# Separate counts for the last group, five parts of one-hots, and 16-bit one-hots of units in a graph-attention and expert kernel

## The chip, the core and the metric

The kernel runs on one core of a Trainium2 chip. The core has five engines that run their own instruction streams side by side: TensorE (matrix products, PE in the profile, with its weight loads as PEld), VectorE (DVE), ScalarE (ACT), GpSimd (POOL) and SyncE (SP, which issues DMAs). Each engine executes its stream in order and waits on semaphores for the others. Products are written to PSUM, everything else works in SBUF, 128 partitions wide. The metric is the device time of one execution in microseconds (us); lower is better.

## What is computed

There are N = 6250 rows of 256 features. The first half is one step of a graph attention, the second a mixture of 8 experts with the best two of each row:

```python
x = x + gnn(layernorm(x))      # per row: 4 heads, softmax over heads, sum over heads
t = layernorm(x)               # the tokens
logits = t @ router_w.T        # [6250, 8]
rw, re = top_k(softmax(logits), 2); rw = rw / rw.sum(-1)
out = t
for e in range(8):
    h = gelu(t @ w1[e] + b1[e])
    out = out + combine[:, e:e+1] * (h @ w2[e] + b2[e])
x = x + out
```

`combine[n, e]` is the share of expert e in row n, and 0 where e isn't one of the two. A row therefore needs only two of the eight experts.

## The kernel before

**First stage.** The rows are cut into 49 tiles of 128, kept in five groups (`GROUPS`: 10, 10, 9, 10 and 10 tiles). For every tile TensorE computes the features of the graph step (`features`, L483) and a table look-up (`look_up`, L508). For every group VectorE then computes the attention (`attend_1` to `attend_3`) and the routing (`route`, L597), which finds the two best experts of each row. Two experts make one of 28 pairs; `mine_all` (L158, 16-bit) holds a one-hot of the pair of each row, 28 values for each tile.

**Sorting.** Rows are then sorted by pair, so that each slice of 128 sorted rows needs few experts. The place of a row is the number of rows of earlier pairs, plus the rows of its pair in earlier tiles, plus those in earlier partitions of its own tile. `rank(g)` (L644) does the last two for a group on TensorE: products of one-hots with a strictly triangular matrix (`before_b`) and with ones (`ones_b`), added up in PSUM, 28 columns for each tile and 28 more for the sum over the whole group. `ranked(g)` (L662) reads these on VectorE: it adds the group's sum to the running `counts`, picks each row's own pair (a product with the one-hot and a sum over pairs), and puts the result into `rank_all`. For groups 0 to 3 this is hidden in the first stage. The last group, z, comes when the first stage is over: L851 to L861 scale its heads on ScalarE (`scaled_heads`), route it, rank it, sum its heads on TensorE (`summed_heads`, whose result ScalarE copies out of PSUM), store its rows to the table in DRAM and call `ranked(z)`.

From L864 on everything is a chain over engines. VectorE turns the counts into `ends`, `starts` and `base` (the first place of each pair in each group), multiplies the base with the one-hots (`ms`, one product for each group), sums over pairs (`place`) and adds `rank_all`. The place is split into a slice (place / 128) and a lane (place % 128).

**Inverting.** The kernel needs for each slice and lane which row stands there. `places(t0, t1)` (L899) makes, for some tiles, 16-bit one-hots of the slice (49 values for each tile) and of the lane (128 values) on VectorE, and two copies of the slice's one-hot, times the row's partition (ScalarE, L906) and times its tile (VectorE, L907). The tile index is innermost in these arrays, with a pitch of 50 values. `placed(t0, t1)` (L910) multiplies them on TensorE, one product of 98 columns for each tile, added up in `pi`. This goes in three parts: tiles 0 to 7, 8 to 23 and 24 to 48, the last with a column of padding. From `pi` VectorE makes `held_by` (L960), the row that each place holds, and GpSimd gathers the rows by it (`fetch`, L982).

**Units.** In parallel VectorE finds which experts each slice takes (`has`, `takes`, `upto`; one small product `pu` between tiles 35 and 36 of `pi`), and numbers the pairs of slice and expert: 125 units. `is_unit` (L954) is a one-hot of each unit's number, 8 experts by 125 units. Sixteen products `pf` (L1001), for the slice and for the expert of each unit and over the 8 experts each, turn it into two lists of 125 numbers. TensorE executes them behind the last product of `pi`. From them come the integer lists from which the engines load registers (`name_units`, L1115).

**Expert loop.** From L1214 on, each of the 125 units takes one slice through one expert: `fill` loads w1 of the expert from DRAM, `first` multiplies and applies the gelu, `second` multiplies with w2 and adds to `acc`. `norm` normalises gathered rows and `turn_slice` transposes them ahead of the loop. `keep_on(26)` (L1005) are 26 products whose result isn't used, on TensorE between pf and the first transpose of a slice.

The order of instructions on every engine is the program's order (a manual schedule); nothing reorders it.

Of the kernel before, what the change touches and what calls it, by code (L numbers as in the profile page):

```python
# [9 lines left out]
FP = mybir.dt.float32  # L10
BF = mybir.dt.bfloat16
I32 = mybir.dt.int32
AF = mybir.ActivationFunctionType
ALU = mybir.AluOpType
# [8 lines left out]
def kernel(  # L23
# [37 lines left out]
    nc = tc.nc  # L61
    N, D = x.shape
    H, OC = attn_l.shape
    NE, _, F = w1.shape
    P = 128
    NT = -(-N // P)
# [3 lines left out]
    GROUPS = [(0, 10), (10, 10), (20, 9), (29, 10), (39, 10)]  # L70
    NG = len(GROUPS)
# [12 lines left out]
    NPAIR = len(PATH)  # L84
    TS = 128
    NS = -(-N // TS)
    NU = 2 * NS + NPAIR - 1
# [22 lines left out]
    ps = ctx.enter_context(tc.tile_pool(name="ps", bufs=2, space=PSUM))  # L110
# [3 lines left out]
    def wide(v, n):  # L114
        return v.rearrange("p (t k) -> p t k", k=1).to_broadcast([v.shape[0], v.shape[1], n])

    def long(v, n):
        return v.rearrange("p (t k) -> p t k", t=1).to_broadcast([v.shape[0], n, v.shape[1]])

    def group(g):  # L120
        return slice(GROUPS[g][0], sum(GROUPS[g]))
# [8 lines left out]
    count_up = const.tile([128, 128], FP, name="count_up")  # L130
# [16 lines left out]
    ones_b = held.tile([128, 128], BF, name="ones_b")  # L147
# [9 lines left out]
    counts = held.tile([P, NG + 1, NPAIR], FP, name="counts")  # L157
    mine_all = held.tile([P, NT, NPAIR], BF, name="mine_all")  # L158
    rank_all = held.tile([P, NT], FP, name="rank_all")
    outside = held.tile([P, 1], FP, name="outside")  # L160
# [3 lines left out]
    NTE = NT + NT % 2  # L164
# [15 lines left out]
    work = early.enter_context(tc.tile_pool(name="work", bufs=2))  # L180
    small = early.enter_context(tc.tile_pool(name="small", bufs=2))
# [39 lines left out]
    for of, pattern, k in ((count_up, [[1, 128]], 0), (number, [[0, 1]], 1)):  # L221
        nc.gpsimd.iota(
            of, pattern=pattern, base=0, channel_multiplier=k,
# [73 lines left out]
    pf = ps.tile([128, NE + 2 * H], FP, name="pf", tag="m")  # L297
# [39 lines left out]
    for c in range(DC):  # L337
        pa = ps.tile([128, 2, H], FP, name="pa", tag="m")
        for k in range(H // 2):
            nc.tensor.matmul(  # L340
                pa, turned_w[2 * c + k], terms[:, k, :, :],
                start=(k == 0), stop=(k == H // 2 - 1),
# [43 lines left out]
    def pair_tables():  # L386

        nc.vector.tensor_scalar(before_b, count_up, number, None, ALU.is_gt)
        nc.vector.tensor_scalar(valid, number, float(LAST), None, ALU.is_lt)

        nc.vector.tensor_scalar(
            outside, number, float(LAST), float(2 * NS * TS), ALU.is_ge, ALU.mult
        )


        for e in range(NE):
            nc.vector.memset(order[:, e : e + 1], 2.0 ** (NE - e))


        one_of = small.tile([P, 2, NPAIR], FP, name="one_of", bufs=1)  # L400
        for i, (a, b) in enumerate(PATH):
            for k, e in enumerate((a, b)):
                nc.vector.memset(one_of[:, k, i : i + 1], float(e))
        for i, (a, b) in enumerate(PATH):
            nc.vector.memset(pairs[:, i : i + 1], 2.0 ** (NE - a) + 2.0 ** (NE - b))

        other = small.tile([NS, NE, NPAIR], FP, name="other", tag="mr", bufs=1)
        for k, to in enumerate((member, other)):
            nc.vector.tensor_tensor(
                to,  # L410
                one_of[:NS, k : k + 1, :].to_broadcast([NS, NE, NPAIR]),
                wide(count_up[:NS, :NE], NPAIR),
                ALU.is_equal,
            )
        nc.vector.tensor_tensor(member, member, other, ALU.add)
        for k in range(2):
            nc.vector.tensor_scalar(
                edge[:, k : k + 1], number[:NS], float(TS), float(k * TS), ALU.mult, ALU.add
            )
# [160 lines left out]
    def summed_heads(g, i, n):  # L580
        pv = ps.tile([P, n, OC], FP, name="pv2", tag="m")
        for h in range(H):
            nc.tensor.matmul(
                pv, ident, pxss[g][:, i : i + n, h * HB : h * HB + OC],
                start=(h == 0), stop=(h == H - 1),
            )
        nc.scalar.copy(xs[g][:, i : i + n, U : U + OC], pv)
# [4 lines left out]
    ranks = {}  # L592

    def store_rows(g):
        nc.sync.dma_start(table_v[:, group(g), :], xs[g])
# [45 lines left out]
            )  # L641
        yield

    def rank(g):  # L644


        n, mine = GROUPS[g][1], mine_all[:, group(g), :]
        pk = ps.tile([P, n + 1, NPAIR], FP, name="rank", tag="r")
        nc.tensor.matmul(pk[:, 0, :], before_b, mine[:, 0, :], start=True, stop=True)
        nc.tensor.matmul(  # L650
            pk[:, 1:, :], ones_b, mine[:, 0:1, :].to_broadcast([P, n, NPAIR]),
            start=True, stop=False,
        )
        nc.tensor.matmul(pk[:, 1:n, :], before_b, mine[:, 1:, :], start=False, stop=False)
        for i in range(1, n):
            nc.tensor.matmul(
                pk[:, i + 1 :, :], ones_b, mine[:, i : i + 1, :].to_broadcast([P, n - i, NPAIR]),
                start=False, stop=(i == n - 1),
            )
        ranks[g] = pk  # L660

    def ranked(g):  # L662
        n, pk = GROUPS[g][1], ranks.pop(g)
        nc.vector.tensor_tensor(
            counts[:, g + 1, :], counts[:, g, :], pk[:, n, :], ALU.add
        )
        mr = small.tile([P, n, NPAIR], FP, name="mr", tag="mr", bufs=1)
        nc.vector.tensor_tensor(mr, pk[:, :n, :], mine_all[:, group(g), :], ALU.mult)
        nc.vector.tensor_reduce(rank_all[:, group(g)], mr, AX.X, ALU.add)
        if g == NG - 1:  # L670
            nc.vector.tensor_tensor(
                rank_all[:, NT - 1 :], rank_all[:, NT - 1 :], outside, ALU.add
            )

# [72 lines left out]
    steps_b = mid.tile([P, TS, CUT], BF, name="steps_b", bufs=1)  # L749
# [49 lines left out]
    for k, (g, b, n) in enumerate(FEATURES):  # L799
# [3 lines left out]
        for j in range(n):  # L803
            i = b + j
# [28 lines left out]
    z = NG - 1  # L833
    n = GROUPS[z][1]
# [9 lines left out]
    warm = small.tile([P, 1], FP, name="warm", bufs=1)  # L844
    nc.scalar.activation(warm, exs[z][:, 0, :1], AF.Gelu)
    rank(z - 1)
    keep_on(8)
    ranked(z - 1)
    attend_2(z)

# [3 lines left out]
    scaled_heads(z, m, n - m)  # L854
    for _ in route(z):
        pass
    rank(z)
    summed_heads(z, 0, m)
    summed_heads(z, m, n - m)
    store_rows(z)  # L860
    ranked(z)  # L861


    count = counts[:, NG, :]  # L864
# [4 lines left out]
    base = small.tile([P, NG, NPAIR], FP, name="base", bufs=1)  # L869
    nc.vector.tensor_tensor(base, counts[:, :NG, :], long(starts, NG), ALU.add)  # L870
    ms = held.tile([P, NT, NPAIR], FP, name="ms", tag="x1")
    for g in range(NG):
        nc.vector.tensor_tensor(
            ms[:, group(g), :], mine_all[:, group(g), :],
            base[:, g : g + 1, :].to_broadcast([P, GROUPS[g][1], NPAIR]), ALU.mult,
        )
    place = small.tile([P, NT], FP, name="place", bufs=1)
# [21 lines left out]
    def places(t0, t1):  # L899

        at, n = slice(t0, t1), t1 - t0
        for to, k, of in ((of_slice, NS, slice_b), (of_lane, TS, lane_b)):
            nc.vector.tensor_tensor(
                to[:, :, at], steps_b[:, :k, :n], long(of[:, at], k), ALU.is_equal
            )
        nc.scalar.activation(by[:, 0, :, at], of_slice[:, :, at], AF.Identity, scale=number)  # L906
        nc.vector.tensor_tensor(  # L907
            by[:, 1, :, at], of_slice[:, :, at], long(count_b[:, at], NS), ALU.mult
        )
    def placed(t0, t1):  # L910
        for t in range(t0, t1):
            nc.tensor.matmul(
                pi, of_lane[:, :, t], by[:, :, :, t], start=(t == 0), stop=(t == NT - 1)
            )

    places(0, 8)
    placed(0, 8)
    places(8, 24)
    placed(8, 24)
    places(24, NTE)  # L920
    placed(24, 36)

    has = small.tile([NS, NPAIR], FP, name="has", bufs=1)
    nc.vector.tensor_scalar(has, ends[:NS], edge[:, 0:1], None, ALU.is_gt)
# [7 lines left out]
    takes = small.tile([NS, NE], FP, name="takes", bufs=1)  # L932
# [4 lines left out]
    nc.vector.tensor_copy(every, upto[:, NE - 1 :])  # L937
    pu = ps.tile([NS, 1], FP, name="pu", tag="r")
    nc.tensor.matmul(pu, before_b[:NS, :NS], every, start=True, stop=True)
    placed(36, NT)  # L940


    fields = small.tile([NS, 2, NE], BF, name="fields", bufs=1)
# [4 lines left out]

    unit = small.tile([NS, NE], FP, name="unit", bufs=1)
    nc.vector.tensor_scalar(unit, upto, pu, float(2 * NU - 1), ALU.add, ALU.add)  # L950
    nc.vector.scalar_tensor_tensor(
        unit, takes, -2.0 * NU, unit, op0=ALU.mult, op1=ALU.add
    )
    is_unit = work.tile([NS, NE, NU], BF, name="is_unit", tag="tT", bufs=4)  # L954
    nc.vector.tensor_tensor(
        is_unit, long(count_up[:NS, :NU], NE), wide(unit, NU), ALU.is_equal
    )
    part_of = small.tile([TS, NS], FP, name="part_of", bufs=1)
    nc.vector.tensor_copy(part_of, pi[:, 0, :])
# [38 lines left out]
    pf = ps.tile([1, 2, NU], FP, name="pf2", tag="r")  # L998
    for k in range(2):
        for e in range(NE):  # L1000
            nc.tensor.matmul(  # L1001
                pf[:, k, :], fields[:, k, e : e + 1], is_unit[:, e, :],
                start=(e == 0), stop=(e == NE - 1),
            )
    keep_on(26)  # L1005
# [8 lines left out]
    for k, of in ((0, 0), (1, 2)):  # L1014
# [4 lines left out]
        op0=ALU.mult, op1=ALU.add,  # L1019
# [194 lines left out]
    for u in range(NU + LAG + 1):  # L1214
# [11 lines left out]
        k, step = divmod(u, 4)  # L1226
# [46 lines left out]
```

## Time and profile before

| | us |
|---|---|
| median of three runs | 416.77 (415.42 to 417.92) |
| the profiled execution, its own time | 419.29 |
| span of its profile | 417.4 |
| TensorE busy | 379.0 (91% of the span) |
| VectorE busy | 306.6 (73%) |
| ScalarE busy | 240.3 (58%) |
| GpSimd busy | 203.1 (49%) |

A busy share is an average over stages. The first stage ends at about 131 us on the profile's time axis, the sorting, inverting and numbering of units lie between 131 and 171 us, and the expert loop takes the rest. In a line of the timeline stand the start in us, the duration in us, the engine, the line of the kernel, the operation, what it writes and reads, the shapes and the number of instructions merged into the line; the bracket at the end is the idle time before it and what ended it. In the chain of waits each piece of time is given to the engine that the end of the run had to wait for. Granted clock is the share of TensorE's full clock that the chip's throttle let through.

### The profile page before, as it was taken

Reading aid. Unit: us, or ns where it says so; the run is one execution under the profiler, and the core shown is the slowest. Engines: PE = TensorE matmul, PEld = TensorE weight load, DVE = VectorE, ACT = ScalarE, POOL = GpSimd, SP = SyncE. Lnnn points to the kernel's source line nnn. Section 1 sums busy time; section 2 is a strip of 40 time slices with the busy share of each in tenths; the row PEclk is TensorE's granted clock in tenths of the full one; section 3 lists DMA queues with packets and bytes.
Section 4 is the critical chain, followed back from the end, with each engine's and each line's share of the span. In section 5 each row is a group of like instructions: output and inputs, shape, how many; then the busy total and the mean of one; then the engine's idle time right before and its main releaser. Section 6 shows DMA issues by size and latency. Waiting matters only on the chain.

```text
span 417.4 us, 9987 instructions
## 1 busy us (share of the span) xinstructions
PE 379.0 (91%) x2599; PEld 327.3 (78%) x2599; DVE 306.6 (73%) x1089; ACT 240.3 (58%) x703; POOL 203.1 (49%) x244
## 2 busy tenths in 40 slices
PE   5999999979894679789999999999999999999990
PEld 4777887767672455679999999999997999999990
DVE  4989839898678795467977877887796887465551
ACT  3477877666573830557667676666765766333330
POOL 0068888899602004444424666766746634233222
PEclk9599999999898676899999999999999999999996
DMA  6974222639823033765667777677777756666520
GB/s 188 355 256 144 77 79 92 239 117 292 270 105 166 0 165 91 230 190 166 198 188 195 206 218 225 220 227 226 224 207 216 202 169 185 192 187 187 165 73 23
DMA packets 53898, 74.66 MB, mean 179 GB/s; under 512 B 7686, under 2 KB 48250, under 8 KB 52948
## 3 DMA queue, kind: packets, MB, share of 16 engines
q1 hardware_dynamic: 46028, 52.45, 40.0%
q0 software_dynamic: 7248, 21.29, 17.2%
q8 instruction: 24, 0.39, 0.4%
q10 hardware_dynamic: 568, 0.27, 0.2%
q14 instruction: 30, 0.25, 0.2%
HBM read 59.13 MB, written 14.87 MB: 177 GB/s over the span
## 4 chain that ended last, share of the span: by engine, by line
PE 50%; POOL 2%; issue 2%; DMA 2%; DVE 1%; ACT 1%; POOLq 0%; DVEq 0%; SPq 0%; ACTq 0%
PE ph L1164 25%; PE py L1180 23%; PE pt L1110 2%; DMA w<-in_L_ffn_w_dram 1%; POOL xr L986 1%; DVE acc L1187 1%; DMA xr<-table,held_by 1%; POOL nm L1067 1%; POOLq L1268 0%; ACT tokT L1111 0%; DVE stats L1061 0%; DVEq L1124 0%; SPq L1152 0%; ACT acc L1087 0%; POOL out_dram L1191 0%
## 5 line engine op out<-in xcount | busy, mean ns | idle before, releaser
L1164 PEld LDWEIGHTS ph<-tokT,w 128*128 128x128 f32 x1000 | 131.5, 193 | 12.5 <-ACT tokT L1111 6.5
L1164 PE MATMUL ph<-tokT,w 128*128 (+1 forms) x1000 | 133.5, 277 | 3.9 <-ACT tokT L1111 3.8
L1180 PE MATMUL py<-big,hid 128*128 x500 | 128.6, 380 | 0.0
L1171 ACT ACTIVATE hid<-ph,b_cols 128x128 f32<-128x128 f32 x250 | 78.4, 364 | 76.8 <-PE ph L1164 76.6
L1180 PEld LDWEIGHTS py<-big,hid 128*128 128x128 f32 x500 | 85.5, 191 | 6.9 <-DVE acc L1187 0.2
L1187 DVE SCALAR_TENSOR_TENSOR acc<-py,shares,acc 128x256 f32 (+1 forms) x125 | 60.5, 484 | 28.0 <-PE py L1180 17.6
L986 POOL DMA_INDIRECT xr<-table,held_by x49 | 49.2, 1004 | 65.0 <-DVE held_by L960 31.6
L1191 POOL DMA_INDIRECT out_dram<-acc,held_out x49 | 50.9, 1039 | 55.2 <-DVE acc L1187 39.7
L1187 DVE SCALAR_TENSOR_TENSOR acc<-big,shares,acc (+1 forms) x125 | 60.1, 481 | 10.5 <-issue 5.2
L487 PE MATMUL px<-w_sb,tT 128*128 128x293 f32 x196 | 56.1, 420 | 0.0
L1077 ACT ACTIVATE tok<-xr,nm 128x256 f32<-128x256 f32 x49 | 29.3, 599 | 33.0 <-DMA w<-in_L_ffn_w_dram 16.0
L487 PEld LDWEIGHTS px<-w_sb,tT 128*128 128x128 f32 x196 | 35.1, 193 | 7.5 <-issue 0.3
L238 POOL DMA_INDIRECT big<-in_x_dram,dst_sb x31 | 34.0, 1097 | 7.3 <-issue 5.9
L495 ACT COPY pxs<-px 128x293 f32<-128x293 f32 x49 | 19.8, 404 | 23.1 <-PE px L487 22.1
L253 ACT COPY tT<-pt 128x512 f32<-128x512 f32 (+2 forms) x56 | 27.1, 528 | 9.6 <-PE pt L249 9.3
L1051 DVE TENSOR_TENSOR xr<-xr 128x512 f32<-128x512 f32 (+1 forms) x25 | 17.2, 690 | 17.0 <-issue 17.0
L1087 ACT ACTIVATE acc<-xr,nm 128x256 f32<-128x256 f32 x49 | 29.1, 596 | 0.0
L1066 POOL TENSOR_SCALAR mv<-mv 128x2 f32<-128x2 f32 (+1 forms) x25 | 5.7, 228 | 35.5 <-DVE mv L1063 34.0
L238 POOL DMA_INDIRECT xd_own<-in_x_dram,dst_sb x18 | 19.1, 1061 | 4.4 <-issue 3.2
L516 PE MATMUL pl<-al_sb,high 128*128 128x196 bf16 x147 | 18.8, 249 | 2.0 <-DVE ag L524 2.0
L1110 PE MATMUL pt<-ident,tok 128*128 128x128 f32 x98 | 19.0, 276 | 1.2 <-ACT tok L1077 1.2
L1067 POOL TENSOR_TENSOR nm<-mv,half_c 128x2 f32<-128x2 f32 (+1 forms) x25 | 18.4, 735 | 2.1
(221 smaller groups left out, 496.1 us busy)
## 6 DMA issues: line engine op xcount, KB each, us to landing
w<-in_L_ffn_w_dram SPq DMA_DIRECT2D x125, 256.0 KB, 3.1
table<-x SPq DMA_DIRECT2D x4, 1685.0 KB
x<-in_x_dram SPq DMA_DIRECT2D x10, 512.0 KB, 9.7
big<-in_L_ffn_w_dram SPq DMA_DIRECT2D x2, 1024.0 KB
high<-highs SPq DMA_DIRECT2D x1, 1568.0 KB
table<-x SPq DMA_DIRECT2D x1, 1516.5 KB
big<-in_L_ffn_b_dram SPq DMA_DIRECT2D x1, 1024.0 KB
xr<-table,held_by POOLq DMA_INDIRECT x49
```

What stands on the lines that cost most here:

```text
L238: nc.gpsimd.indirect_dma_start(out=xd(t), out_offset=None, in_=x[:, :], in_offset=bass.IndirectOffsetOnAxis(ap=dst_sb[:, t : t + 1], axis=0),)
L253: nc.scalar.copy(tT, pt)
L487: nc.tensor.matmul(px, blocks[c][:, k * P : (k + 1) * P], w_sb[:, c, :], start=(c == 0), stop=(c == DC - 1),)
L986: nc.gpsimd.indirect_dma_start(out=xr[:, i, :], out_offset=None, in_=table[:, :], in_offset=bass.IndirectOffsetOnAxis(ap=held_by[:, s0 + i ...
L1077: nc.scalar.activation(tok[:, i, :], xr[:, i, :D], AF.Identity, bias=bias[:, i : i + 1], scale=scale[:, i : i + 1],)
L1087: nc.scalar.activation(acc[:, s * D : (s + 1) * D], xr[:, i, :D], AF.Identity, bias=bias[:, i : i + 1], scale=more[:, i : i + 1],)
L1110: nc.tensor.transpose(pt[:, c, :], tok[:, c * 128 : (c + 1) * 128], ident)
L1164: nc.tensor.matmul(ph[:, j, :], w[:, c * F + j * 128 : c * F + (j + 1) * 128], tokT[:, bass.ds(rows_at + c * TS, TS)], start=(c == 0), sto ...
L1171: nc.scalar.activation(hid[:, j, :], ph[:, j, :], AF.Gelu, bias=b1_cols[:, :, j][:, bass.ds(at_act[u][0], 1)])
L1180: nc.tensor.matmul(py, hid[:, j, :], we2[:, j, bass.ds(at_pe[u][1], D)], start=(j == 0), stop=(j == FC - 1),)
L1187: nc.vector.scalar_tensor_tensor(to, y, share, to, op0=ALU.mult, op1=ALU.add)
L1191: nc.gpsimd.indirect_dma_start(out=ends_at[s][:, :], out_offset=bass.IndirectOffsetOnAxis(ap=held_out[:n, s : s + 1], axis=0), in_=acc[:n, ...
```

## The change

Three things are changed, all between the end of the first stage and the expert loop.

1. **Counts and ranks of the last group.** A new function `all_of` adds up the one-hots of the last group's ten tiles with ten products of 28 columns of their own. `rank` gets an argument `end`; with 0 it leaves out the sum over the whole group, which makes every product with ones 28 columns shorter and drops the last. In place of `ranked(z)` VectorE adds the new sum to the counts. The ranks stay in PSUM: in the loop that makes `ms`, the last group's `base` is added to them, and the sum is multiplied with the one-hot, so that the sum over pairs yields both at once. The last group's columns of `rank_all` are set at the start, to 0 and, for the last tile, to `outside`.
2. **Five parts.** The one-hots of places are made and used in parts of 5, 6, 8, 11 and 19 tiles (20 with the padding) instead of 8, 16 and 25. The small product `pu` comes after tile 37 instead of 35.
3. **One-hots of units.** `unit` is written as 16-bit values, `is_unit` has the expert innermost instead of the unit, and is made by comparing two 16-bit operands (`steps_b`, a table that counts up and that the places use already). The products `pf` read every eighth value of it.

```diff
--- before.py
+++ after.py
@@ -392,6 +392,9 @@
             outside, number, float(LAST), float(2 * NS * TS), ALU.is_ge, ALU.mult
         )
 
+        nc.vector.memset(rank_all[:, group(NG - 1)], 0.0)
+        nc.vector.tensor_copy(rank_all[:, NT - 1 :], outside)
+
 
         for e in range(NE):
             nc.vector.memset(order[:, e : e + 1], 2.0 ** (NE - e))
@@ -641,23 +644,33 @@
             )
         yield
 
-    def rank(g):
+    def rank(g, end=1):
 
 
         n, mine = GROUPS[g][1], mine_all[:, group(g), :]
-        pk = ps.tile([P, n + 1, NPAIR], FP, name="rank", tag="r")
+        pk = ps.tile([P, n + end, NPAIR], FP, name="rank", tag="r")
         nc.tensor.matmul(pk[:, 0, :], before_b, mine[:, 0, :], start=True, stop=True)
         nc.tensor.matmul(
-            pk[:, 1:, :], ones_b, mine[:, 0:1, :].to_broadcast([P, n, NPAIR]),
+            pk[:, 1:, :], ones_b, mine[:, 0:1, :].to_broadcast([P, n + end - 1, NPAIR]),
             start=True, stop=False,
         )
         nc.tensor.matmul(pk[:, 1:n, :], before_b, mine[:, 1:, :], start=False, stop=False)
-        for i in range(1, n):
+        for i in range(1, n + end - 1):
             nc.tensor.matmul(
-                pk[:, i + 1 :, :], ones_b, mine[:, i : i + 1, :].to_broadcast([P, n - i, NPAIR]),
-                start=False, stop=(i == n - 1),
+                pk[:, i + 1 :, :], ones_b,
+                mine[:, i : i + 1, :].to_broadcast([P, n + end - 1 - i, NPAIR]),
+                start=False, stop=(i == n + end - 2),
             )
         ranks[g] = pk
+
+    def all_of(g):
+        n = GROUPS[g][1]
+        pk = ps.tile([P, NPAIR], FP, name="all", tag="r")
+        for i in range(n):
+            nc.tensor.matmul(
+                pk, ones_b, mine_all[:, GROUPS[g][0] + i, :], start=(i == 0), stop=(i == n - 1)
+            )
+        return pk
 
     def ranked(g):
         n, pk = GROUPS[g][1], ranks.pop(g)
@@ -667,10 +680,6 @@
         mr = small.tile([P, n, NPAIR], FP, name="mr", tag="mr", bufs=1)
         nc.vector.tensor_tensor(mr, pk[:, :n, :], mine_all[:, group(g), :], ALU.mult)
         nc.vector.tensor_reduce(rank_all[:, group(g)], mr, AX.X, ALU.add)
-        if g == NG - 1:
-            nc.vector.tensor_tensor(
-                rank_all[:, NT - 1 :], rank_all[:, NT - 1 :], outside, ALU.add
-            )
 
 
 
@@ -854,11 +863,12 @@
     scaled_heads(z, m, n - m)
     for _ in route(z):
         pass
-    rank(z)
+    of_z = all_of(z)
+    rank(z, 0)
     summed_heads(z, 0, m)
     summed_heads(z, m, n - m)
     store_rows(z)
-    ranked(z)
+    nc.vector.tensor_tensor(counts[:, NG, :], counts[:, z, :], of_z, ALU.add)
 
 
     count = counts[:, NG, :]
@@ -870,8 +880,17 @@
     nc.vector.tensor_tensor(base, counts[:, :NG, :], long(starts, NG), ALU.add)
     ms = held.tile([P, NT, NPAIR], FP, name="ms", tag="x1")
     for g in range(NG):
+        of = mine_all[:, group(g), :]
+        if g == z:
+
+            mr = small.tile([P, n, NPAIR], FP, name="mr", tag="mr", bufs=1)
+            nc.vector.tensor_tensor(
+                mr, ranks.pop(z), base[:, z : z + 1, :].to_broadcast([P, n, NPAIR]), ALU.add
+            )
+            nc.vector.tensor_tensor(ms[:, group(z), :], mr, of, ALU.mult)
+            continue
         nc.vector.tensor_tensor(
-            ms[:, group(g), :], mine_all[:, group(g), :],
+            ms[:, group(g), :], of,
             base[:, g : g + 1, :].to_broadcast([P, GROUPS[g][1], NPAIR]), ALU.mult,
         )
     place = small.tile([P, NT], FP, name="place", bufs=1)
@@ -913,12 +932,12 @@
                 pi, of_lane[:, :, t], by[:, :, :, t], start=(t == 0), stop=(t == NT - 1)
             )
 
-    places(0, 8)
-    placed(0, 8)
-    places(8, 24)
-    placed(8, 24)
-    places(24, NTE)
-    placed(24, 36)
+
+    for t0, t1 in ((0, 5), (5, 11), (11, 19), (19, 30)):
+        places(t0, t1)
+        placed(t0, t1)
+    places(30, NTE)
+    placed(30, 38)
 
     has = small.tile([NS, NPAIR], FP, name="has", bufs=1)
     nc.vector.tensor_scalar(has, ends[:NS], edge[:, 0:1], None, ALU.is_gt)
@@ -937,7 +956,7 @@
     nc.vector.tensor_copy(every, upto[:, NE - 1 :])
     pu = ps.tile([NS, 1], FP, name="pu", tag="r")
     nc.tensor.matmul(pu, before_b[:NS, :NS], every, start=True, stop=True)
-    placed(36, NT)
+    placed(38, NT)
 
 
     fields = small.tile([NS, 2, NE], BF, name="fields", bufs=1)
@@ -948,12 +967,13 @@
 
     unit = small.tile([NS, NE], FP, name="unit", bufs=1)
     nc.vector.tensor_scalar(unit, upto, pu, float(2 * NU - 1), ALU.add, ALU.add)
+    unit_b = small.tile([NS, NE], BF, name="unit_b", bufs=1)
     nc.vector.scalar_tensor_tensor(
-        unit, takes, -2.0 * NU, unit, op0=ALU.mult, op1=ALU.add
+        unit_b, takes, -2.0 * NU, unit, op0=ALU.mult, op1=ALU.add
     )
-    is_unit = work.tile([NS, NE, NU], BF, name="is_unit", tag="tT", bufs=4)
+    is_unit = work.tile([NS, NU, NE], BF, name="is_unit", tag="tT", bufs=4)
     nc.vector.tensor_tensor(
-        is_unit, long(count_up[:NS, :NU], NE), wide(unit, NU), ALU.is_equal
+        is_unit, steps_b[:NS, :NU, :NE], long(unit_b, NU), ALU.is_equal
     )
     part_of = small.tile([TS, NS], FP, name="part_of", bufs=1)
     nc.vector.tensor_copy(part_of, pi[:, 0, :])
@@ -999,7 +1019,7 @@
     for k in range(2):
         for e in range(NE):
             nc.tensor.matmul(
-                pf[:, k, :], fields[:, k, e : e + 1], is_unit[:, e, :],
+                pf[:, k, :], fields[:, k, e : e + 1], is_unit[:, :, e],
                 start=(e == 0), stop=(e == NE - 1),
             )
     keep_on(26)
```

## The prediction

> **What bounds the kernel now.** I first read the shares of the chain that ended last: 50% of the span is TensorE, nearly all of it the expert loop from 170.75 us on, which the change leaves alone. So the change can only move the moment at which that loop starts. The timeline of the stretch before it (139 to 171 us), engine by engine, says what sets that moment.
>
> ```profile
> PE 50%; POOL 2%; issue 2%; DMA 2%; DVE 1%; ACT 1%; POOLq 0%; DVEq 0%; SPq 0%; ACTq 0%
> ```
>
> VectorE after the last group's products:
>
> ```profile
> 141.34 0.18 DVE L664 TENSOR_TENSOR counts<-counts,rank 128x28 f32<-128x28 f32 x1 [1.51 <-PE rank L656]
> 141.44 0.44 DVE L668 TENSOR_TENSOR mr<-rank,mine_all 128x280 f32<-128x280 f32 x1
> ...
> 142.48 0.27 DVE L866 TENSOR_TENSOR_SCAN ends<-counts,zero 128x28 f32<-128x28 f32 x1
> ...
> 148.02 0.69 DVE L903 TENSOR_TENSOR of_lane<-steps_b,part 128x1024 bf16<-128x1024 bf16 x1
> ...
> 157.44 1.19 DVE L955 TENSOR_TENSOR is_unit<-count_up,unit 49x1000 bf16<-49x1000 f32 x1
> 159.54 0.21 DVE L959 COPY part_of<-pi 128x49 f32<-128x49 f32 x1 [0.91 <-PE pi L912]
> ...
> 161.31 0.47 DVE L1008 TENSOR_SCALAR which<-pf 1x125 f32<-1x125 f32 x2 [1.31 <-PE pf L1001]
> ...
> 166.37 0.42 DVE L1051 TENSOR_TENSOR xr<-xr 128x256 f32<-128x256 f32 x1 [1.43 <-issue]
> ```
>
> VectorE waits for TensorE at both late steps (0.91 us for pi, 1.31 us for pf). From 161.31 on nothing but its own work and a register load leads to 166.37, then norm, tok, tokT and the loop. So **the end of pf sets the loop's start**, not the gathers (the first is issued at 160.28). TensorE:
>
> ```profile
> 139.62 0.18 PE L649 MATMUL rank<-mine_all,before_b 128*128 128x28 bf16 x1 [4.57 <-DVE mine_all L637]
> ...
> 141.15 6.02 PE L583 MATMUL pv<-pxs,ident 128*128 128x320 f32 x16
> 149.03 1.68 PE L912 MATMUL pi<-by,of_lane 128*128 128x98 bf16 x8 [1.86 <-DVE by L907]
> 151.12 5.70 PE L912 MATMUL pi<-by,of_lane 128*128 128x98 bf16 x28 [0.40 <-DVE by L907]
> 156.75 0.20 PE L939 MATMUL pu<-every,before_b 49*49 49x1 bf16 x1
> 156.88 2.62 PE L912 MATMUL pi<-by,of_lane 128*128 128x98 bf16 x13
> 159.43 1.84 PE L1001 MATMUL pf<-is_unit,fields 49*1 49x125 bf16 x16
> ```
>
> From 149.03 to 161.3 TensorE is busy but for 0.40 us. ScalarE stands between pv and pi:
>
> ```profile
> 147.21 0.43 ACT L587 COPY x<-pv 128x320 f32<-128x320 f32 x1 [1.75 <-PE pv L583]
> 148.19 0.63 ACT L906 ACTIVATE by<-of_slice,number 128x392 bf16<-128x392 bf16 x1 [0.56 <-DVE of_slice L903]
> ```
>
> **Counts by themselves.** The old rank moves 28+280+252+1260 = 1820 columns from 139.62 to 141.15: 1.53 us, 0.84 ns a column at the granted clock of 0.50 that the windows view gives for that stretch. The new order is ten products of 28 columns, then a rank of 28+252+252+1008 = 1540. The smallest old products follow one another in 0.08 to 0.1 us, so the ten take about 0.85 us plus the 0.18 us in which one is finished: VectorE has the counts at 140.65, 0.7 earlier. Between counts and scan the old code had 141.34 to 142.48 = 1.14 us; without L668, L669 and L671 it is 0.22, so 0.9 is gained. In the ms loop the last group's one product (0.38) becomes an addition out of PSUM (as L668: 0.44 and 0.04 before the next) and a product: 0.5 is lost. VectorE reaches the places at 147.75 - 0.7 - 0.9 + 0.5 = 146.65, **1.1 us earlier**. The addition waits for the new rank, which ends near 142, while VectorE gets there at 143.3: no stall. The two writes into rank_all at the start cost 0.1 us of VectorE near 47 us and hide under its 3.94 us wait for POOL's rstd_d at 59.42; without that cover 0.1.
>
> **But TensorE pays for it.** It now spends 0.85 + 1540 x 0.84 = 2.15 us in place of 1.53, so pv starts 0.6 later, at 141.75. pv goes at 0.53 us a product until 143.96 and at 0.27 after, so 4.1 products instead of 5.3 are through by then, and it ends 0.3 later, at 147.5. On ScalarE the second pv copy stands ahead of the first `by`, and pi needs that `by`: copy to 147.95, then `by` for five tiles (0.63 for 392 elements and 0.95 for 784 give 0.82 ns each; 245 take 0.51): pi can start at 148.45. VectorE's first part would have allowed 147.6. So of 1.1 + 0.4 us, about **0.55** reaches TensorE. The store of the last group, issued behind that copy, moves 0.3 too; the gathers come ten microseconds later and cover it.
>
> **Five parts.** The nine operations of the three parts run 147.75 to 154.25. Start to start, of_lane takes 0.60, 1.13 and 1.80 us for 1024, 2048 and 3328 elements: 0.52 ns each and 0.07 fixed. Six more operations add 0.36 us. At that rate the parts are ready at 147.4, 148.3, 149.4, 150.9 and 153.4; TensorE, at 0.20 us a tile from 148.45, wants them at 148.45, 149.45, 150.65, 152.25, 154.45. No gap: the **0.40** goes. The last part leaves 1.1 us of slack, enough for a slowdown of VectorE's first 30 tiles by some 30%. The new starts 5, 11 and 19 and the lengths 5 and 11 are odd; in the trace all of these runs are even, so no row prices this. [...]
>
> So pf starts 0.55 + 0.40 = **0.95 earlier**, at 158.5. pu isn't late: `every` comes at 155.4, tile 38 at 156.2.
>
> **Dense one-hots of units.** VectorE's 1.19 us becomes about 0.6 (1000 x 0.52 + 0.07; runs of 8 as in the first part now). It gains nothing: it ends at 157.5 and pf can't start before TensorE is through pi at 158.5; that work hides it before the change too (158.63 against 159.43). Without that cover 0.6 would be gained. The other side of it: pf used to read 125 adjacent values, and now reads `is_unit[:, :, e]`, every eighth, 16 bytes apart. The two rows that bear on this:
>
> ```profile
> L912 PE MATMUL pi<-by,of_lane x49: 358/366/388, 149.0 to 159.1; 128*128 128x98 bf16 x49
> L1001 PE MATMUL pf<-is_unit,fields x16: 263/308/310, 159.4 to 161.0; 49*1 49x125 bf16 x16
> ```
>
> pi reads 98 values 100 bytes apart and takes longer than pf with 125 adjacent ones. Its pitch is 0.19 us at a granted clock of 0.97 (149 to 151 us) and 0.20 at 0.50, so the array's clock isn't its limit: the spread read is, at 2.0 ns a value. pf's pitch is 1.77/16 = 0.111. At pi's rate 125 values take 0.25, **+2.2 us** over sixteen. From below: 0. From above: half as much again, +3.3, if short steps are worse than pi's long ones. [...] I take the row's 2.2.
>
> **Sum.** -0.95 + 2.2 = +1.25: pf ends at 162.5 instead of 161.3, and the loop starts as much later. The gathers are issued 0.9 earlier, which nobody waits for; keep_on's 26 products shift with pf and still end before tok. The loop itself runs as now. Profiled execution: span 417.4, time 419.29, so 420.5 after. That execution lies 2.5 above the median of the runs shown (416.77); the median is what is compared, so **418.0**.
>
> **Rivals.** (a) The spread read costs pf nothing: -0.95, so 415.8. For it: its step of 16 bytes is far shorter than pi's; against it: pi's row, where a spread read costs whatever the clock. [...] (c) Short steps are worse than long: +2.35, so 419.1. (d) The change frees TensorE of more than I grant, because its clock is up earlier: pv then ends by 146.7 and pi starts at 147.65; with a free pf this is -1.75, so 415.0; with the costly pf about 417.2.
>
> **Numbers.** Forecast with its neighbours 50%, (a) 14%, (b) 20%, (c) 10%, (d) 6%. This kernel's three runs span 2.5 us, so 0.5% (2.1 us) is about the least that tells a change from none. Forecast, (a) and most of (d) lie within it; (b) and half of (c) beyond it, and some of the forecast's own spread of a microsecond: slower 0.32, same 0.61, faster 0.07. The range from 415.2 to 420.9 takes in (a) and (b); the likeliest case's own is 417 to 419.3.
>
> **What would show it.** Right: of_lane for six tiles near 0.47 us; pi without gaps from 148.5; pf's sixteen at 0.25 us each; VectorE waiting for pf some 3 to 4 us. Wrong: pf still at 0.11; of_lane at 0.87 for six tiles with TensorE waiting before each part; or the loop starting with a different wait than register loads behind pf.

## The result, and the profile after

| | before | after |
|---|---|---|
| median of 22 runs each | 415.79 | 417.75 |
| range | 413.79 to 419.14 | 415.23 to 420.48 |
| profiled execution, its own time | 419.29 | 419.18 |
| span of its profile | 417.4 | 417.4 |

The ratio is 1.0044 (95% interval 1.0024 to 1.0065): the change makes the kernel slower by 0.44%, 1.8 us (the medians differ by 1.96), clear of noise and inside the 0.5% that the prediction called no change.

The two profiled spans are equal, and that is chance. The first stage, which the change touches with two tiny writes, ended 1.94 us earlier in the second profile (the last group's `mine_all` starts at 137.17 instead of 139.11 us). In the four other profiles from a chip of like speed (e5, e6, m1 and m2 below), none of which has those writes, it starts anywhere from 135.5 to 138.9. So all stretches below are counted from the start of that `mine_all`, on VectorE; up to it both kernels do the same work but for these writes. Here are the two ends of the stretch, first before the change, then after it:

```profile
139.11 0.45 DVE L637 TENSOR_TENSOR mine_all<-pairs,pair 128x280 bf16<-128x280 f32 x1
...
170.75 3.24 PE L1164 MATMUL ph<-tokT,w 128*128 128x128 f32 x16 [0.46 <-ACT tokT L1111]
```

```profile
137.17 0.45 DVE L640 TENSOR_TENSOR mine_all<-pairs,pair 128x280 bf16<-128x280 f32 x1
...
171.00 2.05 PE L1184 MATMUL ph<-tokT,w 128*128 128x128 f32 x16 [0.46 <-ACT tokT L1131]
```

| us from the start of mine_all to | before | after | change |
|---|---|---|---|
| VectorE adds up the counts | 2.23 | 0.99 | -1.24 |
| first comparison of places | 8.64 | 6.97 | -1.67 |
| first product of pi | 9.92 | 9.08 | -0.84 |
| first product of pf | 20.32 | 20.75 | +0.43 |
| VectorE has pf | 22.20 | 24.49 | +2.29 |
| first product of the expert loop | 31.64 | 33.83 | +2.19 |

Everything gained by the counts is gone by pf, and pf adds the rest. TensorE's timeline of the changed kernel shows where. The second number of a line is the duration of the merged group, the bracket at the end the idle time before it.

```profile
137.67 0.45 PE L670 MATMUL all<-mine_all,ones_b 128*128 128x28 bf16 x10 [4.56 <-DVE mine_all L640]
137.96 0.18 PE L652 MATMUL rank<-mine_all,before_b 128*128 128x28 bf16 x1
...
139.26 6.00 PE L586 MATMUL pv<-pxs,ident 128*128 128x320 f32 x16
146.25 2.47 PE L931 MATMUL pi<-by,of_lane 128*128 128x98 bf16 x11 [0.99 <-ACT by L925]
149.52 3.98 PE L931 MATMUL pi<-by,of_lane 128*128 128x98 bf16 x19 [0.80 <-DVE by L926]
153.76 1.68 PE L931 MATMUL pi<-by,of_lane 128*128 128x98 bf16 x8 [0.27 <-DVE by L926]
155.66 0.16 PE L958 MATMUL pu<-every,before_b 49*49 49x1 bf16 x1 [0.22 <-DVE every L956]
155.75 2.23 PE L931 MATMUL pi<-by,of_lane 128*128 128x98 bf16 x11
157.92 3.71 PE L1021 MATMUL pf<-is_unit,fields 49*1 49x125 bf16 x16
```

Two things stand out. pi, which had one bracketed gap of 0.40 us, now waits for VectorE before the third part, the fifth part and `pu` (the bracketed 0.80, 0.27, 0.22). Shorter waits hide inside merged lines. Followed product by product, starts within a part lie 0.19 us apart; into the second to fifth part the distance is 0.26, 0.97, 0.21 and 0.44 us more than that, 1.9 in all. Before the change it was 0.57 and 0.25 more into the second and third part, 0.8 in all. And pf takes 3.71 us for the same sixteen products that took 1.84. VectorE's timeline names the source of the gaps:

```profile
144.37 0.88 DVE L922 TENSOR_TENSOR of_lane<-steps_b,part 128x640 bf16<-128x640 bf16 x1
145.07 0.45 DVE L926 TENSOR_TENSOR by<-of_slice,count_b 128x245 bf16<-128x245 bf16 x1
...
145.69 1.26 DVE L922 TENSOR_TENSOR of_lane<-steps_b,part 128x768 bf16<-128x768 bf16 x1
146.74 0.61 DVE L926 TENSOR_TENSOR by<-of_slice,count_b 128x294 bf16<-128x294 bf16 x1
...
147.61 1.40 DVE L922 TENSOR_TENSOR of_lane<-steps_b,part 128x1024 bf16<-128x1024 bf16 x1
...
149.70 1.11 DVE L922 TENSOR_TENSOR of_lane<-steps_b,part 128x1408 bf16<-128x1408 bf16 x1
...
151.64 1.49 DVE L922 TENSOR_TENSOR of_lane<-steps_b,part 128x2560 bf16<-128x2560 bf16 x1
...
161.66 0.47 DVE L1028 TENSOR_SCALAR which<-pf 1x125 f32<-1x125 f32 x2 [3.19 <-PE pf L1021]
```

The operation with 1408 values took less time than the one with 1024, and the one with 1024 takes 1.40 us where the same shape took 0.69 before. From start to start, of_lane takes 0.70, 1.05, 1.20, 0.99 and 1.40 us in the five parts; at the rate before the change (0.52 ns a value and 0.07 us an operation, from the 0.60, 1.13 and 1.80 us of its three parts) it would be 0.40, 0.47, 0.60, 0.80 and 1.40. Only the last part, from tile 30 and of even length, runs at that rate. The whole of places takes 9.48 us instead of 6.50. And VectorE now waits 3.19 us for pf instead of 1.31.

### The profile page after: what moved, and what is told of

It is laid out like the page before. It is cut to its first block, busy times and chain, and to the rows that moved or that the text cites. A ratio compares the mean times of both kernels' runs of the same rounds, so it can differ in the third digit from the quotient of the medians.

```text
span 417.4 us, 10011 instructions
## 1 busy us (share of the span) xinstructions
PE 379.9 (91%) x2608; PEld 326.0 (78%) x2608; DVE 308.8 (74%) x1095; ACT 241.1 (58%) x705; POOL 203.1 (49%) x244
## 4 chain that ended last, share of the span: by engine, by line
PE 49%; POOL 2%; issue 2%; DVE 1%; ACT 1%; POOLq 0%; DVEq 0%; ACTq 0%
PE ph L1184 24%; PE py L1200 23%; PE pt L1130 2%; POOL xr L1006 1%; DVE acc L1207 1%; POOL nm L1087 1%; POOLq L1288 0%; ACT hid L1191 0%; DVE stats L1081 0%; DVEq L1144 0%; ACT acc L1107 0%; ACT tokT L1131 0%; POOL out_dram L1211 0%; POOL mv L1086 0%; ACT tok L1097 0%
```

## The experiments

Three theories stood after this. **Mine:** the odd starts and lengths slow VectorE and the spread read slows pf; the two are separate and add up. **First rival:** the gaps come from five parts as such, or from work that happens to lie beside them. **Second rival:** pf is slow for a reason other than its layout. Two more kernels (m1, m2) only measure single operations, in one execution each. Runs e1 to e4 went to a chip on which the kernel before took a median of 429.64 us, e7 to one with 429.91, e5, e6, m1 and m2 to one with 416.01; every ratio is to the kernel before on the same chip.

**e1: the third part undone.**

```diff
-    is_unit = work.tile([NS, NU, NE], BF, ...)
-        is_unit, steps_b[:NS, :NU, :NE], long(unit_b, NU), ALU.is_equal
+    is_unit = work.tile([NS, NE, NU], BF, ...)
+        is_unit, long(count_up[:NS, :NU], NE), wide(unit, NU), ALU.is_equal
-                pf[:, k, :], fields[:, k, e : e + 1], is_unit[:, :, e],
+                pf[:, k, :], fields[:, k, e : e + 1], is_unit[:, e, :],
```

Not shown of the edit: `unit` is written in 32 bits again.

> The changed kernel with its third part undone: is_unit has the unit innermost again and is compared in 32 bits. Measured from the start of the last group's mine_all (VectorE) to the start of pf, and from there to the end of pf: the changed kernel has 20.75 and 3.7 us, the kernel before 20.3 and 1.9. If the spread read makes pf slow, pf falls to 1.9 us and mine_all to the first product of the expert loop from 33.8 to 32.0 us (before: 31.6), so a ratio to the kernel before of about 1.001. If pf is slow for another reason (TensorE's clock, the order of work behind pi), it stays at 3.7 us and the ratio at 1.0045.

```profile
167.71 1.84 PE L1020 MATMUL pf<-is_unit,fields 49*1 49x125 bf16 x16
```

pf is back at 1.84 us (1.88 to VectorE's read), and mine_all to the loop at 32.08 us. Ratio 1.0023 (1.0001 to 1.0045). The layout is what makes pf slow: the order of work was the same, and the granted clock during pf was 0.50 in this run, in the changed kernel and in the kernel before.

**e2: five parts with even bounds.**

```diff
-    for t0, t1 in ((0, 5), (5, 11), (11, 19), (19, 30)):
+    for t0, t1 in ((0, 6), (6, 12), (12, 20), (20, 30)):
```

> The changed kernel with parts of 6, 6, 8, 10 and 19 tiles, so that all starts and lengths are even. If odd starts and lengths slow VectorE, of_lane for 6 tiles takes 0.47 us from start to start instead of 1.05, the nine gaps of TensorE between parts go, and mine_all to pf falls from 20.75 to 19.0 us; ratio to the kernel before 1.001, with pf still at 3.7 us. If five parts by themselves, or the store of the last group's rows that runs at the same time, cause the gaps, mine_all to pf stays near 20.75 and the ratio at 1.0045.

VectorE's and TensorE's timelines of this run, two lines of each:

```profile
152.56 0.56 DVE L922 TENSOR_TENSOR of_lane<-steps_b,part 128x768 bf16<-128x768 bf16 x1
...
154.44 0.69 DVE L922 TENSOR_TENSOR of_lane<-steps_b,part 128x1024 bf16<-128x1024 bf16 x1
```

```profile
154.51 7.26 PE L931 MATMUL pi<-by,of_lane 128*128 128x98 bf16 x38 [0.96 <-DVE of_slice L922]
161.70 0.20 PE L958 MATMUL pu<-every,before_b 49*49 49x1 bf16 x1
```

Six tiles take 0.56 us instead of 1.26, eight 0.69 instead of 1.40, and the 38 products ahead of `pu` run in one piece, their starts nowhere more than 0.2 us apart. (The gaps that the expectation calls nine are four, and the wait of `pu`.) mine_all to pf is 18.62 us, 2.1 less than with odd bounds; pf still takes 3.74. Ratio 1.0009 (0.9985 to 1.0032). Five parts by themselves cost TensorE nothing; on VectorE places takes 6.92 us, the predicted 0.4 above three parts.

**e3: even bounds, and the third part undone** (both edits above).

> Even parts as in the run before, and the one-hots of units as in the kernel before. If the two costs are separate and add up: mine_all to pf 19.0 us, pf 1.9 us, mine_all to the first product of the expert loop 30.3 us against 31.6 before, ratio 0.9968: faster than both kernels. If the two hide each other (the gathers or w1 become the bound once pf is early), the loop starts less than 1 us earlier and the ratio is above 0.998.

```profile
155.02 7.26 PE L931 MATMUL pi<-by,of_lane 128*128 128x98 bf16 x38 [0.96 <-ACT by L925]
...
164.50 1.84 PE L1020 MATMUL pf<-is_unit,fields 49*1 49x125 bf16 x16
```

mine_all to pf 18.75 us, pf 1.88 to VectorE's read, to the loop 30.09: the two costs add up and nothing else becomes the bound. Ratio 0.9962 (0.994 to 0.9983), faster than both kernels.

**e4: the first part of the change alone,** with three parts and the units as before.

> The kernel before with the first part of the change alone (counts of the last group by their own products, ranks added out of PSUM), and with three parts and units as before. VectorE reaches the places 7.0 us after mine_all starts instead of 8.6; the first product of pi is held by ScalarE's copy of pv and its product for 8 tiles, so it starts at 9.3 us instead of 9.9, and the gap of 0.4 us behind the first part goes: mine_all to pf 19.2 us, ratio 0.997. If the new products and the later pv cost TensorE as much as VectorE gains (as my prediction feared in part), mine_all to pf is 20.0 or more and the ratio above 0.999.

```profile
156.85 6.89 PE L931 MATMUL pi<-by,of_lane 128*128 128x98 bf16 x36 [1.04 <-ACT by L925]
```

mine_all to pf 19.06 us, to the loop 30.39; ratio 0.9958 (0.9936 to 0.998). The counts are worth 1.25 us here, and pv starts 2.09 us behind mine_all against 2.04 before, so with the shorter rank their products cost TensorE next to nothing. The gap behind the first part is gone with three parts. Five even parts on top (e3) reach the loop 0.30 us earlier in the trace, but 0.22 of that is pv, which took 6.44 us in e4 and 6.22 in e3 for the same products (at a granted clock of 0.71 and 0.73); the two medians, 428.08 and 427.87, can't be told apart. No gain of the five parts is shown.

**e5: the second part alone,** on the kernel before.

> The kernel before with the second part of the change alone: parts of 5, 6, 8, 11 and 19 tiles. If the odd starts and lengths slow VectorE whatever stands around them, its places take 9.5 us as in the changed kernel instead of 6.5, and mine_all to pf becomes 8.6 + 9.5 + 4.3 = 22.4 us instead of 20.3: ratio 1.005. If the slowness came from work that only the changed order brings beside it (ScalarE's copies, the store of the last rows), the places take 6.9 us and the ratio is 0.999.

```profile
146.33 1.30 DVE L903 TENSOR_TENSOR of_lane<-steps_b,part 128x768 bf16<-128x768 bf16 x1
...
148.24 1.45 DVE L903 TENSOR_TENSOR of_lane<-steps_b,part 128x1024 bf16<-128x1024 bf16 x1
```

Places took 9.41 us and mine_all to pf 22.41; ratio 1.0048 (1.0029 to 1.0067). The slowness follows the odd bounds into another surrounding. The first rival is out.

**e6: the third part alone,** on the kernel before.

> The kernel before with the third part of the change alone. VectorE's is_unit takes 0.67 us instead of 1.19 and pf 3.7 instead of 1.9; nothing but pf is on the path, so mine_all to the first product of the expert loop grows by 1.85 us: ratio 1.0045. If the faster is_unit were worth its 0.5 us: ratio 1.003.

```profile
157.20 0.67 DVE L956 TENSOR_TENSOR is_unit<-steps_b,unit_b 49x1000 bf16<-49x1000 bf16 x1
```

```profile
159.18 3.71 PE L1002 MATMUL pf<-is_unit,fields 49*1 49x125 bf16 x16
```

is_unit took 0.67 us instead of 1.19, pf 3.75 to VectorE's read, and mine_all to the loop 33.39: +1.75. Ratio 1.0054 (1.0025 to 1.0082). The faster comparison brought nothing: VectorE then waited longer for pi (1.42 us instead of 0.91).

**m1: what an odd run costs.** The kernel before with 18 comparisons put in front of the first part, overwritten later:

```diff
+    for n, s_out, s_in, s_step in (...):
+        nc.vector.tensor_tensor(
+            of_lane[:, :, s_out : s_out + n], steps_b[:, :, s_step : s_step + n],
+            long(lane_b[:, s_in : s_in + n], TS), ALU.is_equal,
+        )
```

> The kernel before with 18 more comparisons in front of the first part, each like of_lane (128 runs of n values), all overwritten later: n of 5, 6, 8, 11 and 16 from start 0 and from start 1, and 8 and 16 with only the output, only the place, or only the counting table starting at an odd value. [...] The time isn't compared; some 13 us are added.

Durations in us, 128 runs of n values each, from VectorE's timeline:

| n | all start at 0 | all but the counting table start at 1 | output alone at 1 | either input alone at 1 |
|---|---|---|---|---|
| 5 | 0.83 | 0.88 | | |
| 6 | 0.56 | 1.19 | | |
| 8 | 0.69 | 1.35 | 1.34 | 0.82 |
| 11 | 1.14 | 1.08 | | |
| 16 | 1.23 | 1.57 | 1.56 | 1.36 |

The rows for 16 from 0 and from 1, and for 8 with the output and then one input alone at 1:

```profile
147.79 1.23 DVE L922 TENSOR_TENSOR of_lane<-steps_b,part 128x2048 bf16<-128x2048 bf16 x1
...
153.69 1.57 DVE L922 TENSOR_TENSOR of_lane<-steps_b,part 128x2048 bf16<-128x2048 bf16 x1
155.29 1.34 DVE L922 TENSOR_TENSOR of_lane<-steps_b,part 128x1024 bf16<-128x1024 bf16 x1
156.67 0.82 DVE L922 TENSOR_TENSOR of_lane<-steps_b,part 128x1024 bf16<-128x1024 bf16 x1
```

An odd start doesn't halve the rate whatever the length: 2048 values take 1.57 us, less than the 2.1 us that half the rate of the even rows (twice 0.52 ns a value) would give. Runs of 6 and of 8 lose alike, 0.63 and 0.66 us for 128 runs, so the loss goes by the run rather than by the value; but runs of 16 lose only 0.34, and why was not tried. Most of it is lost at the output: 0.65 us for 128 runs of 8 (5 ns a run) and 0.33 for runs of 16, against 0.13 for an odd input at either length. An odd length costs from an even start too: 5 values take 0.83 us and 11 take 1.14, where the even rows make about 0.49 and 0.89, and for these lengths an odd start changes little. So it is a price for each short run, which for 6 and 8 values about doubles the time (0.56 to 1.19 us, 0.69 to 1.35).

**m2: what a spread read costs.** The 26 unused products of the kernel before replaced by eight groups of six with 125 columns:

```diff
-    keep_on(26)
+    for step in (1, 2, 4, 8, 16, 26):
+        timed(step, 6, ident_b)
+    timed(1, 6, of_lane[:, :, 0])
+    timed(26, 6, of_lane[:, :, 0])
```

> The kernel before with its 26 unused products replaced by groups of six of 125 columns into a scratch: the moving values 1, 2, 4, 8, 16 and 26 values apart (16-bit) with adjacent weights, then 1 and 26 apart with weights that lie 50 values apart. If a spread read costs by the value whatever the step: 0.11 us a product at 1, and 0.23 to 0.25 at every step from 2 on. [...] If pi's 0.2 us for 98 columns came from its spread weights: 0.11 at all steps with adjacent weights, and 0.2 or more with spread ones even at step 1.

TensorE's timeline merges the groups with adjacent weights into one line and those with spread weights into the other:

```profile
157.55 6.12 PE L1012 MATMUL pt<-steps_b,ident_b 128*128 128x125 bf16 x36
163.49 1.86 PE L1012 MATMUL pt<-steps_b,of_lane 128*128 128x125 bf16 x12
```

Followed product by product, starts lie 0.105 us apart at steps of 1 and 2, 0.115 at 4, and 0.22 at 8, 16 and 26 alike. TensorE's granted clock went from 0.50 to 1.00 at 161.1, in the middle of these, and the 0.22 stayed. With spread weights and adjacent values they lie 0.06 apart (at a granted clock of 1.00), with both spread 0.22. So it is the step of the moving operand, the break lies between 8 and 16 bytes, and spread weights cost nothing that shows: at a step of 26 a product takes 0.22 with adjacent weights and with spread ones. Steps of 2 and 4 ran at a granted clock of 0.50 only; what they take at 1.00 was not measured.

**e7: even parts, and 16-bit units with a step of four.**

```diff
-    is_unit = work.tile([NS, NU, NE], BF, ...)
+    is_unit = work.tile([NS, 2, NU, 4], BF, ...)
-                pf[:, k, :], fields[:, k, e : e + 1], is_unit[:, :, e],
+                pf[:, k, :], fields[:, k, e : e + 1], is_unit[:, e // 4, :, e % 4],
```

Not shown of the edit: the even bounds of e2, and the comparison in two operations, one for each half.

> The changed kernel with even parts, and with is_unit in two halves of four experts, still compared in 16 bits: pf then reads values 8 bytes apart instead of 16. By the table of steps (0.11 us a product at a step of 4, 0.22 from 8 on) pf falls from 3.7 to 1.9 us with the 16-bit comparison kept (two operations of 0.33 us), mine_all to pf stays at 18.6 us and mine_all to the first product of the expert loop is 29.8 to 30.1 us: ratio to the kernel before 0.996. If the table doesn't carry over to 49 partitions and one output row, pf stays near 3.7 us and the ratio at 1.001.

```profile
164.49 1.97 PE L1023 MATMUL pf<-is_unit,fields 49*1 49x125 bf16 x16
```

pf took 2.01 us to VectorE's read, the two comparisons 0.79 together, mine_all to the loop 30.46; ratio 0.9966 (0.994 to 0.9993). The table carries over. mine_all to pf was 19.08 us and not 18.6, because pv took 6.55 us here (granted clock 0.69; 6.09 and 0.75 in e2), and pi starts behind it. As the comparison is off the path, this layout gains nothing over e3.

## Why the prediction was right in the result and wrong in one step

- **Which end sets the loop: right.** VectorE waits for pf, and what pf loses arrives at the loop: +2.29 at pf, +2.19 at the loop. e6 shows it by itself: pi ends as before (VectorE reads it 20.41 us behind mine_all, 20.43 before), so the gathers are as early, pf comes 1.85 us later and the loop 1.75. The chain of waits of the profile before does run through the first gather and a load of w, which ends at 169.21. But `tok` starts 0.17 us behind the end of VectorE's `nm` in both profiles (169.03 to 169.20 and 169.28 to 169.45), so the load most likely held nothing up.
- **Counts: right, sized too small.** The ten products start 0.03 us apart (137.67 to 137.96 for all ten), not 0.085. So VectorE had the counts 1.24 us earlier (0.7 predicted) and the places 1.67 (1.1 predicted).
- **TensorE pays: wrong, and without weight.** With 0.29 us instead of 0.85 for the ten and 1.30 for the shorter rank, TensorE spends 1.59 us where 2.15 was predicted and 1.53 spent before: pv starts 2.09 us after mine_all instead of 2.04 and isn't late. ScalarE's copy did hold the first pi as described (0.99 us behind ScalarE's `by`), so of 1.67 us TensorE got 0.84, where 0.55 was predicted.
- **Five parts without a loss: this step failed.** The prediction counted no loss for the odd runs, which no row of the profile before prices: that 0 was the author's estimate. The runs show 2.0 us (mine_all to pf 20.74 in e1, 18.75 in e3, which differ in the bounds alone). Odd runs at half the rate of the even ones don't fit either: at 1.04 ns a value, twice the 0.52, six tiles would take 0.87 us from start to start and eleven 1.53, and they took 1.05 and 0.99 (by m1 the loss goes by the run). That half rate is the (b) of the chances and sets the 420.9 of the range, 2.9 us above the forecast; no run shows one rate for all the odd runs, and the runs showed the 2.0 in its place. The first 30 tiles became 59% slower (6.93 us against 4.36 in e2), past the 30% beyond which the prediction expected TensorE to wait; nearer to 30% nothing was measured.
- **The gap: gone, but not through the five parts.** e4 closes it with three, by the earlier counts alone. The gain was also larger than the bracket's 0.40: from the first product of pi to pf 10.40 us before, 9.49 in e4 and 9.48 in e3. The 0.25 us ahead of the third part were hidden in the merged line of 28 products, where the prediction took TensorE for busy. They also made its 0.20 us a tile at the granted clock of 0.50; product by product it is 0.19 there and at 0.97.
- **Dense units: right.** No gain from VectorE's half microsecond (e6), and pf pays by the spread read: +1.86 us measured, +2.2 predicted. The row of pi gave 2.0 ns a value, this read takes 1.8. m2 has the break between steps of 8 and 16 bytes: a product takes 0.115 us with values 8 bytes apart, where adjacent ones take 0.105 (both at a granted clock of 0.50), and 0.22 with values 16 bytes apart. No step in between was tried.
- **The sum: near by luck.** Predicted was -0.95 + 2.2 = +1.25 us. Measured, pf starts 1.57 earlier with even bounds (18.75 in e3, 20.32 before), the odd bounds cost 1.99 and the spread read 1.86: +2.28, which is the +2.29 of the table. So the forecast change was 1.0 us too small, with 0.6 of gains and 0.3 at pf offsetting a part of the missing 2.0; the medians moved by 1.96. That 418.0 still came so near 417.75 has a second reason: it started from 416.77, the median of three runs, where that of 22 is 415.79. From there the same working gives 417.04.
- **Its own signs.** VectorE waits 3.19 us for pf and pf's products lie 0.22 us apart, near the signs of being right; of_lane at 1.05 us for six tiles, with TensorE waiting before each part, is a sign of being wrong that came true.

## What to carry to other kernels

Cutting these operations into parts was cheap where every part starts and ends on an even 16-bit value: 0.07 us for each of the six added (places took 6.92 us in e2, 6.50 in three parts). At odd bounds the runs of 5 to 11 values took up to 2.2 times as long (of_lane for six tiles 1.05 us from start to start, 0.47 with even bounds). Before turning a layout to please the engine that writes it, price the engine that reads it: here 0.5 us were saved off the path and 1.9 us lost on it. And judge the parts of a change one by one: the first part alone made the kernel 0.4% faster (0.9958), and the other two took back more than that.

## What was not expected of the hardware

- Ten products of 28 columns with the same weights followed one another in 0.03 us each (137.67 to 137.96 in the profile after), at a granted clock of 0.50.
- In m1 the price of an odd start on VectorE went by the run for runs of 6 and 8 values (0.63 and 0.66 us for 128 runs) and sat mainly at the output: 5 ns a run of 8, 2.6 ns a run of 16, about 1 ns for an odd input at either length.
- A moving operand of TensorE with 125 values at steps of 8, 16 and 26 values (16, 32 and 52 bytes) took 1.8 ns a value, 0.22 us a product, at granted clocks of 0.50 and 1.00 (m2). At steps of 2 and 4 values it took 0.105 and 0.115 us at 0.50, and adjacent values 0.105.
- The loop's first sixteen products took 3.2 to 3.5 us in four profiles (before, e1, m1 and m2), at a granted clock of 0.56 to 0.61, and 2.05 us in the other seven, at 1.00. There is one profile of each kernel, so whether an edit decides this is open. Little of it reaches the end: from the loop's first product to the end of the span it is 246.6 us before and 246.4 after. It is a reason to count between points that both kernels share: counted to the end of these sixteen products, the change would have seemed to cost 1.0 us and not 2.2.
